# Modulation gates by way of the outer memory: computed in four column strips, written out, and read back across the partitions ahead of use

## The chip, the cores and the metric

The kernel runs on one core of one Trainium2 chip. The metric is the device time of one execution in microseconds (us). The engines are TensorE (PE; its weight loads are shown as PEld), VectorE (DVE), ScalarE (ACT), GpSimd (POOL) and SyncE (SP), which issues most of the transfers. The four compute engines each run their own instruction queue in order and wait for one another by semaphores.

## The reference

Two transformer blocks over x of shape (4, 1024, 256) in fp32, with 16 heads of width 16. The first block has windowed self-attention, cross-attention to 77 context rows in which each query keeps its 16 largest scores, and a gated MLP. Each of its three branches is multiplied by a gate that is computed from the conditioning vector, one row of 256 numbers for each of the 4 batches:

```python
m = silu(mod) @ w_ada + b_ada                      # (4, 9 * 256)
sh_msa, sc_msa, g_msa, sh_mca, sc_mca, g_mca, sh_mlp, sc_mlp, g_mlp = [m[:, i*C:(i+1)*C][:, None, :] for i in range(9)]
h = _self_attn(_ln(x) * (1 + sc_msa) + sh_msa, w_qkv, b_qkv, w_so, b_so)
x = x + h * g_msa
h = _topk_cross_attn(_ln(x) * (1 + sc_mca) + sh_mca, context, w_q, b_q, w_kv, b_kv, w_co, b_co)
x = x + h * g_mca
h = _swiglu(_ln(x) * (1 + sc_mlp) + sh_mlp, w_m1, b_m1, w_m2, b_m2)
x = x + h * g_mlp
```

The second block is plain cross-attention to the same context with its own modulation and without a gate.

## The kernel before

The work is cut into 16 units, four of 256 rows in each of 4 batches, and each unit goes through five stages: self-attention, the selection of the 16 largest scores, cross-attention, the MLP and the last attention. All operations of all units are first recorded, each with an engine, a cost, a priority and the buffers it reads and writes. A planner (`Plan.place`) then simulates the engines with these costs and picks an order; `issue` emits the instructions in that order, in one stream, so the recorded function of an operation puts all its instructions, whichever engine they belong to, at that operation's place in the order. Buffers come from small rings: two PSUM banks (`mm`) for nearly all dense products, two places for `gate`, two each for `w_so` and `w_co`, one for `w_m2`. A table of priorities (`ORDER`, `AHEAD`, `NUDGE`) shapes the plan.

A gate multiplies the columns of an output projection, so the kernel scales the weights once for each batch instead of every unit's result. `mod_gate` makes gate i for all 4 batches: two products of the conditioning (4 rows) with 256 columns of `w_ada` (L727), and a VectorE addition of the bias (L730) into `gates`, which has 4 partitions. `gated(b, ...)` then prepares batch b's three weights. For each, `w_so`, `w_co` or `w_m2` and its bias row are loaded, TensorE spreads the gate's row over 128 partitions by a product with a repeated column of the identity (L1303), ScalarE copies it from PSUM to one of the two `gate` places (L1306), and GpSimd multiplies the bias row (L1308) and the weight (L1310) by it. So there are 12 gates in all, 3 for each batch.

Other lines that matter below: L1011 and L1023 are GpSimd's steps of the normalization of an attention result, with ScalarE's L1008, L1013 and L1018 and VectorE's L1025 between them; L1035 is the output projection that uses the scaled weight; L1049 is GpSimd's addition of the scaled bias row to x; L907 and L909 are GpSimd's part of a layer norm; L961 to L965 split a shift into bf16 parts for TensorE (L970); L699 makes the other modulation rows, 32 columns of the array at a time in four strips; L821 is a layer norm of the context at the start; L1335 emits spare products where the plan has TensorE idle.

Of the kernel before, what the change touches and what calls it, by code (L numbers as in the profile page):

```python
# [9 lines left out]
F32 = mybir.dt.float32  # L10
BF16 = mybir.dt.bfloat16
AF = mybir.ActivationFunctionType
ALU = mybir.AluOpType
# [3 lines left out]
P = 128  # L17
# [371 lines left out]
def tile_block(ctx: ExitStack, tc: tile.TileContext, a: dict, out: bass.AP):  # L389
    nc = tc.nc  # L390

    x_d, cond_d, ctx_d = a["x"], a["cond_1024"], a["ctx_1024"]
    B, L, C = x_d.shape
# [3 lines left out]
    KC = C // P  # L397
# [21 lines left out]
    ident = ctile([P, P], "ident")  # L419
# [25 lines left out]
    for i in range(3):  # L445
        t = ctile([P, TU, 4, 32], f"parts{i}", BF16)
# [5 lines left out]
    for i in range(2):  # L452
        t = ctile([P, TU, H // 2, VP], f"v_self{i}")
# [3 lines left out]
    pl = Plan()  # L457
# [5 lines left out]
    def f_act(n):  # L463
        return 0.21 + 0.00081 * n

    def f_dve(n):
        return 0.155 + 0.00104 * n

    def f_pool(n):
        return 0.13 + 0.00222 * n  # L470
# [7 lines left out]
    T_GATE = ("D", "D", 0.22, 0.05, 0.37, 0.216)  # L478
# [11 lines left out]
    def fixed(name, shape, dt=F32):  # L490
        return pl.fixed(ctile(shape, name, dt), name)
# [7 lines left out]
    bp = fixed("bp", [P, C])  # L499
    n_mod = 26  # L500
    mod = fixed("mod", [P, n_mod, B])
    gates = fixed("gates", [B, 3, C])
    k_ctx = [fixed(f"k_{i}", [P, KC, B, 2, LC]) for i in range(2)]
    v_ctx = [fixed(f"v_{i}", [LC, B, H // 2, VP]) for i in range(2)]
    for v, fill in zip(v_ctx, (0.0, 1.0)):
# [7 lines left out]
    start, total = {}, 0  # L513
# [45 lines left out]
    at = Place(0)  # L559
# [3 lines left out]

    sc_t = at.buf("sc_t", [P, KC, 32])
    nc.gpsimd.memset(sc_t(), 0.0)
    bg_ada = at.buf("bg_ada", [B, 3, C])
    cx = at.buf("cx", [LC, B, C])
    cn = at.buf("cn", [LC, B, C])
    w_kv = [at.buf("w_kv0", [P, KC, 2 * C])]
# [3 lines left out]
    at = Place(start["slab"])  # L573
# [15 lines left out]
    def load(buf, src, kb, prio, key=None, eng="SP", view=None):  # L589
        def fn():  # L590
            dst = buf() if view is None else view(buf())
            (nc.sync if eng == "SP" else nc.scalar).dma_start(dst, src)
        pl.op(eng, f_dma(kb) if eng == "SP" else 0.3, fn, w=[buf if key is None else (buf, key)],
              prio=prio, lag=2.0)
# [8 lines left out]
    def row_bc(buf, name, lo, prio, key=None, view=None, np_=P):  # L603
        load(buf, a[name][lo : lo + C].partition_broadcast(np_), np_, prio, key, view=view)
# [11 lines left out]
    for g, names in enumerate(groups):  # L616
        for name, hi in names:
            n, r = hi // P, n_rows[g]
# [2 lines left out]
            col_of[name] = (g, r)  # L621
            n_rows[g] += n
    for i in range(3):
        row_bc(bg_ada, "L0_xcond_b_ada", (3 * i + 2) * C, (-79.5, -59.5, -49.5)[i], i, lambda t, i=i: t[:, i, :], B)
    row_bc(bv_self, "L0_xcond_b_qkv", 2 * C, -81)
    row_bc(bv_ctx[0], "L0_xcond_b_kv", C, -66)
    row_bc(bv_ctx[1], "L1_xcond_bkv", C, -29.5)
# [57 lines left out]
        nc.scalar.preload_act_table_set("natural_log_exp_and_others")  # L685
    pl.op("ACT", 1.5, silu, w=[sc_t], r=[pc], prio=-50, lag=-1.28)

    turn = [0]

    def mod_group(name, lo, m, scale_first, prio, dma_prio):  # L690
# [30 lines left out]
    def mod_gate(i, prio, dma_prio):  # L721
        c = chunk("L0_xcond_w_ada", (3 * i + 2) * C, C, dma_prio)
        pp = pl.buf("mm", f"modg{i}")

        def fn():
            for kc in range(KC):
                nc.tensor.matmul(pp()[:B, :C], sc_t()[:, kc, :B], c()[:, kc, :C],  # L727
                                 start=(kc == 0), stop=(kc == KC - 1))
        pl.op("PE", f_pe(C, 2), fn, w=[pp], r=[sc_t, c], prio=prio)
        pl.op("DVE", f_dve(256), lambda: nc.vector.tensor_tensor(  # L730
            gates()[:, i, :], pp()[:B, :C], bg_ada()[:, i, :], ALU.add), w=[(gates, i)], r=[pp, (bg_ada, i)], prio=prio)

    def filled(v):

# [67 lines left out]
    for q in range(4):  # L802
        lo = (q % 2) * HID + (q // 2) * 4 * P
# [7 lines left out]
    for b in range(B):  # L811
        pl.op("DVE", 0.42, lambda b=b: nc.vector.bn_stats(st_c()[:LC, b, :], cx()[:, b, :]),
              w=[(st_c, b)], r=[cx], prio=-1)
    for b in range(B):
        pl.op("DVE", 0.16, lambda b=b: nc.vector.bn_aggr(mv_c()[:LC, b, :], st_c()[:LC, b, :]),
              w=[(mv_c, b)], r=[(st_c, b)], prio=-1)
# [475 lines left out]
    def gated(b, pr):  # L1292

        gw = {}
        for i, (key, name, kc) in enumerate(
            (("so", "L0_xcond_w_so", KC), ("co", "L0_xcond_w_co", KC), ("m2", "L0_xcond_w_m2", NF))
        ):
            first = None if b else DMA_FIRST[i]
            w, row = pl.buf("w_" + key, f"w_{key}{b}"), pl.buf("row", f"b_{key}{b}")
            gate, pg = pl.buf("gate", f"gate{b}{i}"), pl.buf("mm", f"pg{b}{i}")  # L1300
            load(w, a[name].rearrange("(kc p) n -> p kc n", p=P), 128 * kc, first or pr)
            load(row, a[f"L0_xcond_b_{key}"].partition_broadcast(P), 128, first or pr)
            pl.op("PE:gate", T_GATE, lambda i=i, pg=pg: nc.tensor.matmul(  # L1303
                pg()[:, :C], ident[:B, b : b + 1].to_broadcast([B, P]), gates()[:, i, :], start=True, stop=True),
                w=[pg], r=[(gates, i)], prio=pr, take=[gate])
            pl.op("ACT:gate", f_act(256), lambda gate=gate, pg=pg: nc.scalar.copy(gate(), pg()[:, :C]),  # L1306
                  w=[gate], r=[pg], prio=pr)
            pl.op("POOL:gate", f_pool(256), lambda row=row, gate=gate: nc.gpsimd.tensor_tensor(  # L1308
                row(), row(), gate(), ALU.mult), w=[row], r=[row, gate], prio=pr)
            pl.op("POOL:gate", f_pool(256 * kc), lambda w=w, gate=gate, kc=kc: nc.gpsimd.tensor_tensor(  # L1310
                w(), w(), gate().unsqueeze(1).to_broadcast([P, kc, C]), ALU.mult),
                w=[w], r=[w, gate], prio=pr)
            gw["b_" + key], gw["w_" + key] = row, w
        return gw

# [60 lines left out]
```

## Time and profile before

| | |
|---|---|
| Median of 3 runs | 1040.41 us (1040.08 to 1044.87) |
| The profiled execution | 1041.43 us, span of its instructions 1039.4 us |
| TensorE busy, share of the span | 97%; VectorE 73%, ScalarE 70%, GpSimd 52% |
| Transfers | 27.01 MB, nearly all on SP's queue; DMA engines 70% busy in the first 52 us, then mostly idle |
| TensorE clock by fortieths of the span | 0.9 of full in the first slice, 0.7 in the second, then 0.9 or more |

In the profile, a line such as L1303 is the line of the kernel's source that recorded the instruction. A count such as x24 is of instructions; an fp32 product appears as two. What stands behind an arrow in brackets is the event that ended the idle time in front of an instruction. Busy times of TensorE include waiting inside its pipeline, so that a busy share near 100% shows that its queue is never empty, not that it works at its peak.

### The profile page before, as it was taken

To read this page: it belongs to the slowest core of one execution; us is meant where nothing else is said; L and a number is where in the kernel's file an instruction comes from. 1 tells how busy PE (TensorE), PEld (TensorE's weight loads), DVE (VectorE), ACT (ScalarE), POOL (GpSimd) and SP (SyncE) were. 2 spreads that over 40 slices of the span, in tenths; PEclk is the share of its full clock that TensorE was granted. 3 is DMA by queue.
4 is the path that set the end of the run, shared out by engine and by line. 5 is a ranking of instruction groups with operands and counts; after the bars stand their busy time and mean duration, and the time that the engine had idled before them with its cause. 6 is when DMAs were issued, how large, how long until landed. Compare 5 with 4: busy or idle time off the path is not lost.

```text
span 1039.4 us, 27476 instructions
## 1 busy us (share of the span) xinstructions
PE 1012.0 (97%) x10363; PEld 770.5 (74%) x10363; DVE 757.3 (73%) x4000; ACT 723.5 (70%) x1270; POOL 542.1 (52%) x751
## 2 busy tenths in 40 slices
PE   7899999999999999999999999999999999999997
PEld 5667777777777778777877777778767787778775
DVE  5177999979899999947833446599999977724232
ACT  3358786687687794758468667877688765764665
POOL 3384445466353573557635647546335464753653
PEclk9799999999999999999999999999999999999999
DMA  7710000001000000100000200000000001000000
GB/s 255 242 50 7 3 2 1 3 3 36 3 22 27 7 3 5 38 16 22 21 1 2 82 22 21 2 2 2 2 2 22 2 2 42 12 1 12 2 21 21
DMA packets 23623, 27.01 MB, mean 26 GB/s; under 512 B 1609, under 2 KB 20675, under 8 KB 23491
## 3 DMA queue, kind: packets, MB, share of 16 engines
q1 hardware_dynamic: 23455, 25.26, 7.7%
q8 instruction: 81, 1.33, 0.5%
q14 instruction: 52, 0.42, 0.1%
q10 hardware_dynamic: 35, 0.01, 0.0%
HBM read 21.07 MB, written 4.19 MB: 24 GB/s over the span
## 4 chain that ended last, share of the span: by engine, by line
PE 48%; DVE 13%; ACT 6%; POOL 2%; issue 1%; POOLq 0%; ACTq 0%; DVEq 0%
PE mm L1247 13%; PE mm L1275 8%; PE mm L938 5%; PE mm L1035 5%; PE s L1196 4%; PE o L1212 3%; PE s L985 3%; DVE share L1153 2%; DVE r L1147 2%; DVE nm L996 2%; PE s L1186 1%; DVE share L1145 1%; DVE share L1151 1%; PE mm L919 1%; ACT prob L1108 1%
## 5 line engine op out<-in xcount | busy, mean ns | idle before, releaser
L1247 PE MATMUL mm<-share,w_m 128*128 128x256 f32 x640 | 150.3, 386 | 0.4 <-ACT share L926 0.2
L1205 ACT ACTIVATE prob<-s 77x2048 f32<-77x2048 f32 x64 | 120.0, 1875 | 43.7 <-PE s L1201 43.4
L996 DVE TENSOR_REDUCE nm<-s 128x16 f32<-128x2048 f32 (+1 forms) x64 | 119.0, 1859 | 38.0 <-PE s L985 17.2
L1247 PEld LDWEIGHTS mm<-share,w_m 128*128 128x128 f32 x640 | 117.7, 190 | 26.0 <-issue 4.7
L1147 DVE MATCH_REPLACE8 r<-share 128x77 f32<-128x77 f32 x512 | 109.9, 222 | 0.0
L1145 DVE MAX8 share<-share 128x8 f32<-128x77 f32 x512 | 94.4, 225 | 21.0 <-ACT share L1138 21.0
L1153 DVE MATCH_REPLACE8 share<-share,r 128x77 f32<-128x77 f32 x512 | 109.6, 221 | 0.0
L1011 POOL TENSOR_TENSOR share<-share 128x256 f32<-128x256 f32 x64 | 47.1, 736 | 96.4 <-ACT share L1008 95.1
L1151 DVE MAX8 share<-r 128x8 f32<-128x77 f32 x512 | 93.9, 224 | 0.0
L1247 PE MATMUL mm<-slab,w_m 128*128 128x256 f32 x384 | 92.9, 388 | 0.7 <-ACT slab L926 0.5
L1023 POOL TENSOR_TENSOR slab<-slab,share 128x256 f32<-128x256 f32 x96 | 69.4, 730 | 28.4 <-ACT share L1018 19.2
L1261 POOL TENSOR_SCALAR slab<-slab 128x512 f32<-128x512 f32 x43 | 64.4, 1498 | 36.8 <-ACT slab L1259 33.0
L1247 PEld LDWEIGHTS mm<-slab,w_m 128*128 128x128 f32 x384 | 69.9, 190 | 15.6 <-issue 3.1
L1275 PE MATMUL mm<-share,slab 128*128 128x256 f32 x344 | 80.9, 381 | 0.0
L1008 ACT ACTIVATE share<-o,mask 128x256 f32<-128x256 f32 x128 | 66.6, 575 | 12.2 <-PE o L1212 9.6
L1108 ACT ACTIVATE prob<-s 128x2048 f32<-128x2048 f32 x32 | 60.5, 1889 | 17.9 <-PE s L1104 17.5
L1044 DVE TENSOR_TENSOR slab<-slab,mm 128x512 f32<-128x512 f32 x52 | 35.4, 680 | 50.9 <-PE mm L1035 25.7
L1275 PEld LDWEIGHTS mm<-share,slab 128*128 128x128 f32 x344 | 64.7, 190 | 10.0 <-issue 0.9
L1253 ACT ACTIVATE slab<-mm,cols 128x256 f32<-128x256 f32 x90 | 43.0, 480 | 41.0 <-PE mm L1247 40.5
L1212 PE MATMUL o<-prob,v 77*32 77x256 f32 x1024 | 67.9, 385 | 0.8 <-ACT share L1018 0.5
L1049 POOL TENSOR_TENSOR slab<-slab,row 128x512 f32<-128x512 f32 x39 | 49.9, 1278 | 28.5 <-DVE slab L912 15.4
L907 POOL TENSOR_SCALAR rs<-mv 128x2 f32<-128x2 f32 x64 | 14.2, 222 | 81.7 <-DVE mv L905 78.8
(183 smaller groups left out, 2427.0 us busy)
## 6 DMA issues: line engine op xcount, KB each, us to landing
share<-in_L_xcond_w_m_dram SPq DMA_DIRECT2D x4, 1024.0 KB
slab<-in_x_dram SPq DMA_DIRECT2D x9, 256.0 KB, 2.9
out_dram<-slab SPq DMA_DIRECT2D x9, 256.0 KB, 2.7
w_m<-in_L_xcond_w_m_dram SPq DMA_DIRECT2D x4, 512.0 KB, 6.8
share<-in_L_xcond_w_ada_dram SPq DMA_DIRECT2D x3, 512.0 KB, 3.8
w_so<-in_L_xcond_w_so_dram SPq DMA_DIRECT2D x4, 256.0 KB
w_co<-in_L_xcond_w_co_dram SPq DMA_DIRECT2D x4, 256.0 KB, 4.0
w_qkv<-in_L_xcond_w_qkv_dram SPq DMA_DIRECT2D x3, 256.0 KB
```

Source lines behind the costliest of these rows:

```text
L996: pl.op("DVE:max", f_dve(n), lambda: nc.vector.tensor_reduce(nm()[:, t], s4(), AX.X, ALU.max, negate=True), w=[(nm, t)], r=[s], prio=u.prio)
L1008: pl.op("ACT:nln", 0.5, lambda e=e, own=own, other=other: nc.scalar.activation(nz()[:, e, :], o()[:, ts(e, UT)], AF.Ln, bias=own, scale=ot ...
L1023: nc.gpsimd.tensor_tensor(dst, dst, shaped(nz()[:, k, :], dst), op)
L1108: pl.op("ACT:exp", f_act(2048), lambda s=s, prob=prob: nc.scalar.activation(prob(), s(), AF.Exp), w=[prob], r=[s], prio=pr)
L1145: nc.vector.max(top()[:, h + i, 0:8], sc()[:, h + i])
L1147: nc.vector.match_replace(r1()[:, i], top()[:, h + i, 0:8], sc()[:, h + i], NEG)
L1151: nc.vector.max(top()[:, h + i, 8:16], r1()[:, i])
L1153: nc.vector.match_replace(sc()[:, h + i], top()[:, h + i, 8:16], r1()[:, i], NEG)
L1205: pl.op("ACT:exp", f_act(2048), lambda s=s, prob=prob: nc.scalar.activation(prob()[:LC], s()[:LC], AF.Exp), w=[prob], r=[s], prio=pr)
L1212: nc.tensor.matmul(o()[r, :UT] if drops is not None else o()[r, ts(e, UT)], columns(v_z()[:, b], 8 * c + 2 * j + e), prob()[:LC, j, ts(e, ...
L1247: nc.tensor.matmul(pp()[:, ts(half, UT)], w_m1()[:, kc, m : m + P], ht()[:, kc, :], start=(kc == 0), stop=(kc == KC - 1))
L1275: nc.tensor.matmul(pp()[:, ts(t, C)], gts[f // 2]()[:, f % 2, ts(t, P)], w_m2()[:, f, :], start=(f == 0), stop=(f == NF - 1))
```

## The change

A gate is made in four column strips. The conditioning's 32 (padded) columns are multiplied with 64 columns of `w_ada` at a time, and strip j's result stands in partitions 32j to 32j + 3 of one PSUM tile; the bias, loaded in the same layout, is added to all 128 partitions at once. Right behind that addition, in the same recorded operation, GpSimd's queue gets four writes, one for each strip, to a tile of its own in the outer memory (`gates_d[i]`, 4 x 256). TensorE's spreading and ScalarE's copy stay in the plan with their costs, but emit nothing. In their stead GpSimd's queue reads the gate's row from the outer memory into all 128 partitions of the place that the plan gave it: the first two gates right after their writes, every later one as soon as the second multiplication by the gate that held the same place has been issued. The order of all other operations is the planner's, as before.

```diff
-    gates = fixed("gates", [B, 3, C])
+    gates = fixed("gates", [P, 3, C // 4])
+    dram = ctx.enter_context(tc.tile_pool(name="dram", bufs=1, space=bass.MemoryType.DRAM))
+    gates_d = [dram.tile([B, C], F32, tag=f"gates_d{i}", name=f"gates_d{i}") for i in range(3)]
...
-    bg_ada = at.buf("bg_ada", [B, 3, C])
+    bg_ada = at.buf("bg_ada", [P, 3, C // 4])
...
-        row_bc(bg_ada, "L0_xcond_b_ada", (3 * i + 2) * C, (-79.5, -59.5, -49.5)[i], i, lambda t, i=i: t[:, i, :], B)
+        lo = (3 * i + 2) * C
+        load(bg_ada, a["L0_xcond_b_ada"][lo : lo + C].rearrange("(j o n) -> j o n", j=4, o=1).to_broadcast([4, 32, C // 4]),
+             B, (-79.5, -59.5, -49.5)[i], i, view=lambda t, i=i: t[:, i, :])
...
+    gate_of = {}
+
+    def read_gate(n, place):
+        todo = [m for m in range(n, 3 * B) if gate_of[m]() is place]
+        if todo:
+            b, i = divmod(todo[0], 3)
+            nc.gpsimd.dma_start(place, gates_d[i][b, :].partition_broadcast(P))
...
             for kc in range(KC):
-                nc.tensor.matmul(pp()[:B, :C], sc_t()[:, kc, :B], c()[:, kc, :C],
-                                 start=(kc == 0), stop=(kc == KC - 1))
+                for j in range(4):
+                    nc.tensor.matmul(pp()[32 * j : 32 * j + 32, : C // 4], sc_t()[:, kc, :], c()[:, kc, ts(j, C // 4)],
+                                     start=(kc == 0), stop=(kc == KC - 1))
         pl.op("PE", f_pe(C, 2), fn, w=[pp], r=[sc_t, c], prio=prio)
-        pl.op("DVE", f_dve(256), lambda: nc.vector.tensor_tensor(
-            gates()[:, i, :], pp()[:B, :C], bg_ada()[:, i, :], ALU.add), w=[(gates, i)], r=[pp, (bg_ada, i)], prio=prio)
+
+        def add():
+            nc.vector.tensor_tensor(gates()[:, i, :], pp()[:, : C // 4], bg_ada()[:, i, :], ALU.add)
+            for j in range(4):
+                nc.gpsimd.dma_start(gates_d[i][:, ts(j, C // 4)], gates()[32 * j : 32 * j + B, i, :])
+            if i < 2:
+                read_gate(i, gate_of[i]())
+        pl.op("DVE", f_dve(256), add, w=[(gates, i)], r=[pp, (bg_ada, i)], prio=prio)
...
-            pl.op("PE:gate", T_GATE, lambda i=i, pg=pg: nc.tensor.matmul(
-                pg()[:, :C], ident[:B, b : b + 1].to_broadcast([B, P]), gates()[:, i, :], start=True, stop=True),
-                w=[pg], r=[(gates, i)], prio=pr, take=[gate])
-            pl.op("ACT:gate", f_act(256), lambda gate=gate, pg=pg: nc.scalar.copy(gate(), pg()[:, :C]),
-                  w=[gate], r=[pg], prio=pr)
-            pl.op("POOL:gate", f_pool(256), lambda row=row, gate=gate: nc.gpsimd.tensor_tensor(
-                row(), row(), gate(), ALU.mult), w=[row], r=[row, gate], prio=pr)
-            pl.op("POOL:gate", f_pool(256 * kc), lambda w=w, gate=gate, kc=kc: nc.gpsimd.tensor_tensor(
-                w(), w(), gate().unsqueeze(1).to_broadcast([P, kc, C]), ALU.mult),
-                w=[w], r=[w, gate], prio=pr)
+            gate_of[3 * b + i] = gate
+            pl.op("PE:gate", T_GATE, lambda: None, w=[pg], r=[(gates, i)], prio=pr, take=[gate])
+            pl.op("ACT:gate", f_act(256), lambda: None, w=[gate], r=[pg], prio=pr)
+            uses = []
+
+            def times_gate(t, g, n=3 * b + i, gate=gate, uses=uses):
+                nc.gpsimd.tensor_tensor(t, t, g, ALU.mult)
+                uses.append(t)
+                if len(uses) == 2:
+                    read_gate(n + 1, gate())
+            pl.op("POOL:gate", f_pool(256), lambda row=row, gate=gate, times_gate=times_gate: times_gate(row(), gate()),
+                  w=[row], r=[row, gate], prio=pr)
+            pl.op("POOL:gate", f_pool(256 * kc), lambda w=w, gate=gate, kc=kc, times_gate=times_gate: times_gate(
+                w(), gate().unsqueeze(1).to_broadcast([P, kc, C])), w=[w], r=[w, gate], prio=pr)
```

## The prediction

> **What bounds the kernel now.** I read the page first, then busy time by stretches, then the gate's own lines, then POOL in order of time, since POOL is where the change puts its new work.
>
> Page, busy time of each engine:
>
> ```profile
> PE 1012.0 (97%) x10363; PEld 770.5 (74%) x10363; DVE 757.3 (73%) x4000; ACT 723.5 (70%) x1270; POOL 542.1 (52%) x751
> ```
>
> Stretches (length, then busy of PE, PEld, DVE, ACT, POOL, then TensorE clock, DMA share, GB/s):
>
> ```profile
> 35.00:65.00 30.00, 28.44 (x243) 21.00 (x243) 10.62 (x38) 17.54 (x37) 21.12 (x23) 0.77 0.63 200
> 65.00:130.00 65.00, 62.39 (x816) 48.22 (x818) 57.38 (x253) 47.51 (x88) 33.12 (x55) 1.00 0.02 6
> 250.00:350.00 100.00, 97.41 (x1081) 72.37 (x1084) 95.73 (x562) 73.92 (x125) 44.08 (x75) 1.00 0.07 20
> 500.00:600.00 100.00, 98.96 (x951) 74.29 (x950) 46.78 (x157) 64.18 (x113) 54.11 (x74) 1.00 0.07 24
> ```
>
> TensorE is the bound, but DVE is nearly full too until about 350 us; after that TensorE stands alone. Between 35 and 65 us the clock is low and POOL, with 21.1 of 30 us, is busier than DVE or ACT.
>
> The lines of the gate's matmul and of its copy:
>
> ```profile
> L1303 PE MATMUL mm<-gates,ident x24: 372/454/791, 34.5 to 563.7; 4*128 4x256 f32 x24
> L1306 ACT COPY gate<-mm x12: 354/372/530, 35.2 to 567.4; 128x256 f32<-128x256 f32 x12
>   POOL row L1308: 22.4, 6
> ```
>
> Twelve gates, two matmul instructions and one copy each, all in the first 568 us; the last row says POOL waited 22.4 us, in six pieces, for those copies.
>
> POOL in order of time (start, length; in brackets its idle time before and who ended it):
>
> ```profile
> 23.88 0.26 POOL L965 TENSOR_TENSOR parts<-rest,parts 128x32 bf16<-128x32 f32 x1
> 35.63 0.72 POOL L1308 TENSOR_TENSOR row<-row,gate 128x256 f32<-128x256 f32 x1 [11.50 <-DMA w_m<-in_L_xcond_w_m_dram]
> ...
> 46.80 0.72 POOL L1308 TENSOR_TENSOR row<-row,gate 128x256 f32<-128x256 f32 x1
> 52.09 0.73 POOL L1011 TENSOR_TENSOR share<-share 128x256 f32<-128x256 f32 x1 [4.56 <-ACT share L1008]
> ...
> 55.36 0.86 POOL L1011 TENSOR_TENSOR share<-share 128x256 f32<-128x256 f32 x1 [1.44 <-ACT share L1008]
> ...
> 59.34 3.02 POOL L1023 TENSOR_TENSOR slab<-slab,share 128x256 f32<-128x256 f32 x4
> ```
>
> POOL is free from 24.1 to 35.6, multiplies three gates until 47.5, idles 4.6 us, then runs almost without a gap from 55.4 to 62.4, and TensorE's first output projection (L1035) starts at 63.8 after it. So POOL has some 4.6 + 1.4 us of slack ahead of a place where it sets TensorE's time.
>
> **The change part by part.** Numbers are against this execution (span 1039.4, its time 1041.43 us, 0.1% above the median 1040.41). About 0.5% (5.2 us) is what a measurement of this kernel can tell from no change.
>
> *TensorE loses the twelve gate matmuls.* From the timeline, start of the pair to start of what follows, less what the neighbour takes elsewhere: 0.58 (at 89.9), 0.41 (103.7), 0.35 (117.5), 0.62 (271.3), 0.53 (336.1), 0.53 (507.3), 0.63 (527.8), 0.62 (563.4): 4.3 us for eight. The five before 350 us (2.5) lie where DVE is nearly full; I take half, 1.25. The three after (1.8) I take at nine tenths, 1.6. Together -2.8; the ends are 0 (another engine is late instead) and -4.3. The four early gates (34.5 to 43.3) run at the low clock, about 0.85 and 1.0 us for the third and fourth on the way to the first weighted sums at 49.1; those 1.8 us count only if POOL is ready then (below).
>
> *ACT loses twelve copies* (12 x 0.372 = 4.5 us). Hidden behind TensorE where TensorE is the bound; where ACT's head waited for a gate (4.64 us at 507.9) the next work waits for the same TensorE order. I count 0; at best 1 us.
>
> *The three gates are computed in strips.* Before, four instructions in 0.8 to 1.0 us; the strips of L699 (16 instructions, 128 columns) take 0.64, so with 64 columns at most that. DVE's addition goes from 0.41 to some 0.2 (64 columns for 256). At 10 to 31 us these lie beside loads (TensorE still waits 1.4 us for a weight at 33.1): 0; without that cover -1. The bias loads become 128 pieces of 256 bytes: three issues on SP go from 0.27-0.39 to about the 0.47 of a 128-partition row load, +0.4 us on SP, which pauses from 20 to 29 anyway: 0, at worst +0.3. The smaller bias tile also moves the setup tiles behind it in the shared space; their last readers are done by 38.5 us, long before the rings laid over them are used: 0.
>
> *POOL issues 12 writes and 12 reads.* This is the disputed cost. No POOL DMA is in the trace. Nearest rows: SP's issues, 0.23 to 0.47 us each, and landing times of 2.5 to 2.9 us from issue (out_dram<-slab 2.5 and 2.7, slab<-in_x 2.9), 4.6 to 9.3 when the queues are full. The Trainium skill, "DMA: Bandwidth & Descriptors", section "SWDGE vs HWDGE vs iDMA", says that a DMA from GpSimd has its descriptors computed by that engine's own cores, where SP's are made by hardware; its section "Latency and other measured facts" prices the first at about 1 us ahead of the first byte, against 0.6. It speaks against this change, and no run here shows it. SP's row is another mechanism, so I take c = 1.0 us of POOL per DMA (an estimate from that page; ends 0.4 and 1.5), and l = 3 us to land (the write rows, a little more because the DMA share at 32 to 44 us is 0.88 to 0.99).
>
> The first gate is harmless: its addition ends at 11.8, POOL is idle until 20.7, and 5c + l = 8. Gates two and three are not. Their additions end at 29.8 and 31.4. POOL's queue then holds, in order: four writes, the read (which waits until they have landed, and everything behind it on POOL with it), four writes of the third gate, and only then the multiplication that now starts at 35.63. It starts at 29.85 + 9c + l = 41.85. The work up to the third row (POOL's own 10.4 us, the additions of L1049 included) now contains three reads: done at 40.25 + 12c + l = 55.25, where it was 47.5. The 4.6 us of slack is gone; the first L1011 starts at 55.25 instead of 52.09, and who waits for it are ACT's L1013, DVE's L1025 and then L1023. The second L1011 follows 1.7 us later (56.95 for 55.36); the run of 7.0 us to the end of L1023 gets one more read, ending at 64.95 where it was 62.36: **+2.6 us** at TensorE's first projection, which later work inherits almost whole. With c = 0.4, l = 2.5 POOL is ready at 47.6, the chain starts as early as TensorE allows, and this becomes -1.8 + 0.4 = -1.4; with c = 1.5 it is +9.1. It turns from gain to loss near c = 0.8.
>
> *Later reads.* Six, each about 1 us of POOL right behind the weight's multiplication. At 424 and 533 POOL has 6.4 and 1.5 us of idle time behind: 0. At 96.6 the next L1011 is 0.8 late, with 1.8 idle after it: +0.3. At 237.9, 0.55 idle ahead of a queue: +0.2. At 335.2 the read comes 2.0 us before its use at 337.25; it lands near 338.8, and L961 at 338.93, on which TensorE waits, goes to 339.5: +0.5. At 510.4 L907 is 1.0 late: +0.3. Together +1.3, ends +0.3 and +2.5. What replaces the 22.4 us of POOL's waits for the copies is mostly nothing, as the reads are old by then (9 of 12 by over 9 us); POOL just idles further on, so 0.
>
> Sum: -2.8 + 2.6 + 1.3 = +1.1 us, hence 1041.5 on the median.
>
> A second rule bears on the loss. The Trainium skill, "TensorE: Matmul & The Clock Gate", Part 1, says that an idle window of about 3.4 us halves the clock until a busy one has passed. Here the clock is 0.50 at 36 to 48 us though TensorE counts as busy for all of 40 to 48, so recovery takes longer than the rule says. A stall of 2.6 us at 63 us would cost nothing more by the rule; one of 9 us would cost 2 to 5 us on top.
>
> **The rivals.** *Faster (0.20):* POOL's issues cost what SP's do. Then -1.4 early, TensorE's full -4.3, later +0.3, ACT -0.5: -5.9, that is 1034.5. For it: after 500 us TensorE is 99% busy with nothing else near it. Against: DVE's 95.7 of 100 us where five gates lie.
> *Slower (0.35):* POOL's queue at 29.8 us is the bound. From c = 1.3 the early term is +6.5 or more and the total passes +5; at c = 1.5 it is +8, with the clock up to +13, about 1050. Its far end: if each strip's write waits for the landing of the one before (their rows in the outer memory interlace), a gate costs 4(c + l) = 16 us of POOL and the first multiplication starts past 70, some +30: 1070. For it: the queue is in order and the slack only 6 us. Against: the strips' addresses are disjoint.
> *It does not do what it says (0.03):* the reads stand so close to their use that POOL waits for them as it did for copies; true of 335 us alone by the order above, +0.5 each, still about 1042.
>
> **How the numbers follow.** The likeliest case (0.42) has c between 0.6 and 1.25: 1037.5 to 1045.5, point 1041.5; with the third rival 0.45 within 0.5%. Faster 0.20, slower 0.35. For 8 in 10 the range takes most of the faster case (to 1033.5) and the slower one without its far end (to 1053).
>
> **What would show it.** L1303 and L1306 gone from TensorE and ACT; POOL DMA rows of about 1 us; the first L1308 near 42; the first L1011 near 55; L1035 near 66 with TensorE idle before it; after 500 us the stretch shorter by 1 to 2 us. L1308 before 37 would make the slow step wrong; L1308 past 50 would make the forecast too low.

## The result and the profile after

The changed kernel takes 1049.18 us (median of 4 runs, 1048.32 to 1050.61), the kernel before 1040.63 us (4 runs, 1040.08 to 1044.87): a ratio of 1.0081, 95% interval 1.0062 to 1.0100. It is slower by more than the 0.5% that can be told from no change. The spans of the two profiled executions, 1047.5 and 1039.4 us, differ by 8.1 us, and this is what has to be explained.

The first part of the page says little: TensorE lost 5.8 us of busy time and POOL gained 14.7 us.

```profile
PE 1006.2 (96%) x10375; PEld 768.4 (73%) x10375; DVE 760.0 (73%) x4000; ACT 720.2 (69%) x1258; POOL 556.8 (53%) x775
```

(The 24 spreading instructions are gone from TensorE, but the strips of the gates brought 36 new ones.) Two stretches say where to look. Columns: length, busy time of PE, PEld, DVE, ACT, POOL, TensorE clock, DMA share, GB/s:

```profile
35.00:65.00 30.00, 20.10 (x211) 14.97 (x212) 7.36 (x28) 13.83 (x27) 21.13 (x24) 0.73 0.68 219
65.00:130.00 65.00, 61.56 (x755) 48.28 (x754) 56.91 (x249) 43.95 (x80) 37.99 (x60) 1.00 0.04 10
```

Between 35 and 65 us TensorE was busy for 20.1 of 30 us instead of 28.4, and POOL was as busy as before: POOL did its work, but at other times.

To find the rest I matched the instructions of the two traces, one by one for each engine, and took start after less start before. The difference, of single profiled executions:

| at (us of before) | after less before | what happens there |
|---|---|---|
| 45 to 50 | -2 to -2.7 (TensorE) | TensorE ahead, without the gates' products |
| 60, then 64 | +6.2, +5.5 | POOL late at the first normalization (L1034) |
| 64 to 236 | +5.5, constant | the spreading products at 89.9, 103.7 and 117.5, now gone, give nothing |
| 240, 260 | +8.6, +7.6 | one subtraction of VectorE, see below |
| 340, 364 | +8.4, +8.8 | POOL waits for the read of a gate, see experiment 2 |
| 507 | +8.0 | the product at 507.3 gone: -0.8 |
| to the end | +8.0 | the products at 527.8 and 563.4 give nothing |

The lines of the source have moved: in the changed kernel L751 issues the writes of a gate and L702 the reads, L1333 is both multiplications by a gate (L1308 and L1310), L1034 and L1046 are the steps of the normalization (L1011 and L1023), L1072 is the addition of the bias row (L1049), L930, L932 and L935 are the layer norm (L907, L909 and L912), and L806 is VectorE's bias addition that takes a product of the context out of PSUM (L783). In the kernels of the experiments they move by a few lines more.

The DMAs of the change, issue durations (min/median/max, ns) and landing:

```profile
L751 POOL DMA_DIRECT2D gates_d<-gates x12: 515/521/767, 11.9 to 39.9; - x12
L702 POOL DMA_DIRECT2D gate<-gates_d x12: 582/635/654, 19.9 to 532.9; - x12
gates_d<-gates POOLq DMA_DIRECT2D x12, 1.0 KB, 6.1
gate<-gates_d POOLq DMA_DIRECT2D x12, 128.0 KB, 3.3
```

A write occupies POOL for 0.52 us and a read for 0.64, but a write of 1 KB needs a median of 6.1 us to land. What that does shows in POOL in order of time, in the stretch that the prediction was about (start, length; in brackets the idle time before and who ended it):

```profile
30.01 2.16 POOL L751 DMA_DIRECT2D gates_d<-gates  x4 [5.91 <-DVE gates L749]
37.77 0.58 POOL L702 DMA_DIRECT2D gate<-gates_d  x1 [5.61 <-DMA gates_d<-gates]
38.34 2.05 POOL L751 DMA_DIRECT2D gates_d<-gates  x4
40.41 0.74 POOL L1333 TENSOR_TENSOR row<-row,gate 128x256 f32<-128x256 f32 x1
41.10 1.27 POOL L1333 TENSOR_TENSOR w_so<-w_so,gate 128x512 f32<-128x512 f32 x1
46.75 0.62 POOL L702 DMA_DIRECT2D gate<-gates_d  x1 [4.38 <-DMA bp<-in_L_xcond_bp_dram]
...
55.95 0.73 POOL L1333 TENSOR_TENSOR row<-row,gate 128x256 f32<-128x256 f32 x1
56.97 0.58 POOL L702 DMA_DIRECT2D gate<-gates_d  x1 [0.30 <-POOL row L1333]
57.57 0.73 POOL L1034 TENSOR_TENSOR share<-share 128x256 f32<-128x256 f32 x1
58.40 0.23 POOL L930 TENSOR_SCALAR rs<-mv 128x2 f32<-128x2 f32 x1
58.71 0.73 POOL L932 TENSOR_TENSOR rs<-rs,mhalf 128x2 f32<-128x2 f32 x1
```

There are two waits of a read for its own gate's writes, with everything else of POOL behind each: 5.61 us at 32.2, and 4.38 us at 42.4. The second is put down to a load (`bp`), which the trace shows landing at 46.69. The third gate's last write was issued at 39.87 and landed at 46.18, so at least 3.8 of the 4.38 us are the wait for the writes.

Who waits for POOL there is not only the normalization. L932 is the step of the next unit's layer norm, and VectorE's queue stands behind it:

```profile
51.93 0.42 DVE L806 TENSOR_TENSOR v<-mm,share 77x256 f32<-77x256 f32 x1 [2.61 <-ACT k L794]
59.48 1.13 DVE L935 TENSOR_SCALAR slab<-slab,mv,rs 128x256 f32<-128x256 f32 x2 [7.13 <-POOL rs L932]
60.52 0.41 DVE L806 TENSOR_TENSOR v<-mm,share 77x256 f32<-77x256 f32 x1
```

The second L806 would free a PSUM bank for TensorE, but it is queued behind L935, which waits for POOL. So TensorE has nothing to do from 53.6 to 61.0 us:

```profile
60.99 1.11 PE L942 MATMUL mm<-ident,slab 128*128 128x128 f32 x4 [7.43 <-DVE v L806]
```

And its clock falls (columns as in the stretches above):

```profile
44.00:48.00 4.00, 4.00 (x87) 3.17 (x86) 1.06 (x3) 1.45 (x1) 1.24 (x2) 0.94 0.99 309
56.00:60.00 4.00, 0.00 (x0) 0.00 (x0) 0.53 (x1) 0.42 (x1) 3.51 (x7) 0.77 0.42 117
60.00:64.00 4.00, 3.01 (x9) 2.30 (x10) 2.82 (x12) 1.44 (x3) 3.31 (x4) 0.50 0.01 2
```

The first of these rows shows the side of the change that works: TensorE has its clock back at 44 to 48 us, where the trace of before shows 0.50 until 48. The gain is spent on waiting for POOL.

The second step, at 240 us, is a single instruction of VectorE, the subtraction behind the selection of the 16 largest scores. Before, VectorE and then the POOL instruction beside it, which began while the subtraction ran and took 0.90 us instead of 0.73:

```profile
240.26 0.41 DVE L1158 TENSOR_TENSOR share<-share 128x256 f32<-128x256 f32 x1
```

```profile
240.36 0.90 POOL L1011 TENSOR_TENSOR share<-share 128x256 f32<-128x256 f32 x1
```

After, VectorE and then POOL at the same time:

```profile
245.71 3.58 DVE L1181 TENSOR_TENSOR share<-share 128x256 f32<-128x256 f32 x1
```

```profile
243.62 0.65 POOL L702 DMA_DIRECT2D gate<-gates_d  x1 [0.30 <-POOL w_so L1333]
244.30 1.28 POOL L1072 TENSOR_TENSOR slab<-slab,row 128x512 f32<-128x512 f32 x1
245.54 0.73 POOL L1046 TENSOR_TENSOR slab<-slab,share 128x256 f32<-128x256 f32 x1
246.23 0.72 POOL L1034 TENSOR_TENSOR share<-share 128x256 f32<-128x256 f32 x1
246.91 0.72 POOL L1046 TENSOR_TENSOR slab<-slab,share 128x256 f32<-128x256 f32 x1
247.60 0.72 POOL L1034 TENSOR_TENSOR share<-share 128x256 f32<-128x256 f32 x1
248.29 0.72 POOL L1046 TENSOR_TENSOR slab<-slab,share 128x256 f32<-128x256 f32 x1
```

The subtraction starts inside an unbroken run of POOL and ends 0.28 us after the run does. The read at 243.6 stands 2.1 us ahead of the subtraction. The Trainium skill, "SBUF — State Buffer", section "Who interferes with whom", says that a VectorE instruction with two operands in SBUF and a GpSimd instruction that reads SBUF lock each other out for a whole instruction, and that the order of issue decides who waits. The trace of before agrees: the subtraction there ends 0.28 us after the POOL instruction that it began beside. After the change it waits for five instructions, not one.

### The profile page after: what moved, and what is told of

Read it like the earlier page. It is cut to its first block, busy times and chain, and to the rows that moved or that the text cites. A ratio compares the mean times of both kernels' runs of the same rounds, so it can differ in the third digit from the quotient of the medians.

```text
span 1047.5 us, 27517 instructions
## 1 busy us (share of the span) xinstructions
PE 1006.2 (96%) x10375; PEld 768.4 (73%) x10375; DVE 760.0 (73%) x4000; ACT 720.2 (69%) x1258; POOL 556.8 (53%) x775
## 4 chain that ended last, share of the span: by engine, by line
PE 44%; DVE 15%; ACT 5%; POOL 3%; issue 2%; DMA 1%; POOLq 0%; ACTq 0%; DVEq 0%
PE mm L1270 12%; PE mm L1298 7%; PE mm L961 5%; PE mm L1058 5%; PE s L1219 3%; PE o L1235 3%; PE s L1008 3%; DVE r L1170 3%; DVE share L1176 3%; DVE share L1168 2%; DVE share L1174 2%; PE mm L942 1%; PE s L1209 1%; PE mm L1098 1%; DVE slab L935 1%
## 5 line engine op out<-in xcount | busy, mean ns | idle before, releaser
L1034 POOL TENSOR_TENSOR share<-share 128x256 f32<-128x256 f32 x64 | 46.9, 733 | 86.3 <-ACT share L1031 81.7
L1046 POOL TENSOR_TENSOR slab<-slab,share 128x256 f32<-128x256 f32 x96 | 69.6, 732 | 38.6 <-ACT share L1041 19.1
L1072 POOL TENSOR_TENSOR slab<-slab,row 128x512 f32<-128x512 f32 x39 | 49.9, 1280 | 30.2 <-DVE slab L935 17.1
L930 POOL TENSOR_SCALAR rs<-mv 128x2 f32<-128x2 f32 x64 | 14.3, 224 | 91.7 <-DVE mv L928 88.9
```

The costliest lines, as they stand in the source:

```text
L1046: nc.gpsimd.tensor_tensor(dst, dst, shaped(nz()[:, k, :], dst), op)
```

## The experiments

Two explanations were to be tested. The one of the early stretch (theory 1 in the expectations): the transfers cost about 6 to 7 us because POOL's queue stands behind reads that wait for slowly landing writes, while the removal of products and copies is worth some 3 to 5 us by itself. The one of the step at 240 us (theory 3): a read that is issued by POOL moves POOL's instructions so that they hold VectorE's subtraction. All shifts below are starts against the profiled execution of before, as in the table above. The first four kernels were timed against a median of before of 1042.09 us (7 runs), the next three against 1041.95 us (39 runs), the last against 1041.07 us (27 runs).

**1. The changed kernel without its transfers.** The 24 DMAs are left out, and with them the gates' values: both places are filled with ones.

```diff
-            for j in range(4):
-                nc.gpsimd.dma_start(gates_d[i][:, ts(j, C // 4)], gates()[32 * j : 32 * j + B, i, :])
-            if i < 2:
-                read_gate(i, gate_of[i]())
+            if i == 0:
+                for n in range(2):
+                    nc.gpsimd.memset(gate_of[n](), 1.0)
...
-                if len(uses) == 2:
-                    read_gate(n + 1, gate())
```

> The changed kernel without its 24 transfers: both gate places are filled once with ones, so the multiplications by the gates use ones. It shows what taking the matmuls and copies away is worth when nothing takes their place. Theory 1 (the loss is POOL's in-order queue between 30 and 50 us; TensorE's freed time is worth nothing after 65 us, as the two traces keep a constant distance there): the work near 62 us starts 1 to 2.5 us earlier than in the kernel before, and nothing is gained later but about 1 us near 507: 1037 to 1039.5. The prediction's view (freed TensorE time carries): 4 to 5 us, 1036 or less.

Measured: 1036.76 us (1036.01 to 1037.43), ratio 0.9954 (0.9938 to 0.9971); span 1033.9, 5.5 us below before. The shift is -4.4 us already by 52 us, stays there but for small steps, goes to -5.6 at 508 and ends at -5.5. So the removal is worth 5.5 us of span, of which 4.4 come from the four early gates and about 1 from the eight later ones: between the two expected values, larger early and smaller late than I had it. The windows show the early part, in the low-clock stretch:

```profile
40.00:44.00 4.00, 4.00 (x64) 3.22 (x64) 0.09 (x1) 1.88 (x1) 2.39 (x1) 0.79 1.05 362
44.00:48.00 4.00, 4.00 (x80) 2.85 (x76) 2.09 (x7) 3.25 (x5) 3.24 (x3) 1.00 0.91 246
```

Before, the same two windows:

```profile
40.00:44.00 4.00, 4.00 (x47) 3.26 (x46) 0.00 (x0) 2.00 (x2) 3.82 (x3) 0.50 0.88 305
44.00:48.00 4.00, 4.00 (x27) 2.90 (x30) 0.50 (x1) 0.51 (x2) 3.53 (x2) 0.50 0.83 259
```

TensorE's clock returns some 7 us earlier. Why taking away eight small instructions does this was not tested. POOL is ready too: its first normalization starts at 47.61 (52.09 before).

**2. The kernel before with the transfers added.** Gates by TensorE and ScalarE as before; the same 12 writes and 12 reads on POOL, the reads into 96 partitions that nothing uses.

```diff
+            for j in range(4):
+                nc.gpsimd.dma_start(gates_d[i][:, ts(j, C // 4)], gates()[:B, i, ts(j, C // 4)])
+            if i < 2:
+                read_gate(i, gate_of[i]())
...
+                if len(uses) == 2:
+                    read_gate(n + 1, gate())
```

> The kernel before with the 24 transfers added on POOL's queue at the same places; the reads go to 96 spare partitions that nobody uses, and the gates still come from TensorE and ACT. Theory 1 (POOL's queue): POOL waits twice for writes to land, the first multiplication starts near 40, the third row ends near 56, and the first projection (66 in the changed kernel) is 5 to 6 us late; with the step near 240 us the total is 1046 to 1050. Rival (strips, bias loads or the missing TensorE work cause the loss): 1040 to 1042, since none of these is in this kernel.

Measured: 1048.78 us (1047.88 to 1049.38), ratio 1.0067 (1.0052 to 1.0082); span 1046.6. The shift is +6.2 at 64 us, +8.2 at 240, and 7.2 from 272 us to the end: both steps of the change are here, with no strips and no product removed. POOL waits in the same two places:

```profile
39.00 0.54 POOL L698 DMA_DIRECT2D gates<-gates_d  x1 [6.05 <-DMA gates_d<-gates]
...
48.61 0.57 POOL L698 DMA_DIRECT2D gates<-gates_d  x1 [5.07 <-DMA bp<-in_L_xcond_bp_dram]
```

So the transfers bring both steps by themselves. The third loss of the change, +1.2 at 335 to 364 us, is not here: the shift stays at 7.2. There the changed kernel waits for the read itself, which was issued at 343.32, too close to its use:

```profile
346.64 0.72 POOL L1333 TENSOR_TENSOR row<-row,gate 128x256 f32<-128x256 f32 x1 [2.66 <-DMA gate<-gates_d]
```

In this kernel the gate comes from ScalarE, and POOL waits 1.41 us for it. The two parts do not add up (-5.5 and +7.2 make +1.7, the change has +8.1), above all since early, where POOL is the bound, TensorE's lead is worth only 6.2 - 5.5 = 0.7 us instead of 4.4; the rest is this third loss and a step at 240 us of 1.0 us net here and 2.1 there.

**3. The second gate's read behind the first gate's multiplications.** The two multiplications by the first gate then stand ahead of the wait.

```diff
-            if i < 2:
-                read_gate(i, gate_of[i]())
+            if i == 0:
+                read_gate(0, gate_of[0]())
...
                 if len(uses) == 2:
+                    if n == 0:
+                        read_gate(1, gate_of[1]())
                     read_gate(n + 1, gate())
```

> The changed kernel with one move: the read of the second gate is issued behind the first gate's two multiplications instead of ahead of them, so that the four writes of the third gate and the first multiplications do not stand behind the wait for the second gate's writes. The number of transfers is the same. Theory 1 (waiting for the landing costs, not issuing): the first row is multiplied near 34.5 to 36 instead of 40.4, the third row is done near 51, the early loss of 5.5 us becomes 0 or a gain of up to 2; the step near 240 stays or not by chance of phase: 1039 to 1043. Rival (issuing 24 transfers on POOL is the cost): 1046 or more, as all are still issued.

Measured: 1047.2 us (1046.22 to 1047.27), ratio 1.0050 (1.0035 to 1.0065); span 1045.5. Early the shift is +3.5 us, where theory 1 had expected none: a miss. The trace shows why:

```profile
34.03 0.74 POOL L1333 TENSOR_TENSOR row<-row,gate 128x256 f32<-128x256 f32 x1
...
37.32 0.62 POOL L702 DMA_DIRECT2D gate<-gates_d  x1 [1.34 <-DMA gates_d<-gates]
39.06 0.56 POOL L702 DMA_DIRECT2D gate<-gates_d  x1 [1.11 <-DMA gates_d<-gates]
44.66 0.72 POOL L1333 TENSOR_TENSOR row<-row,gate 128x256 f32<-128x256 f32 x1 [5.05 <-DMA gate<-gates_d]
```

The waits for writes are down to 1.34 and 1.11 us, and the first multiplication is at 34.0, as expected. But then the read itself takes 7.3 us from issue to use (37.32 to 44.66), and POOL waits 5.05 us for it. The rival's number (1046 us or more) came true, its cause (the time for issuing) did not: the issues take 0.52 to 0.62 us each, and POOL stands idle. It is the round trip, write and read, of 12 to 14 us under the loads that has to fit ahead of the second gate's use. The step at 240 us is here as well: +7.0 after 3.8, the subtraction at 3.57 us.

**4. All transfers on SP's queue.** The reads stand where the plan has the spreading product.

```diff
-                nc.gpsimd.dma_start(gates_d[i][:, ts(j, C // 4)], gates()[32 * j : 32 * j + B, i, :])
+                nc.sync.dma_start(gates_d[i][:, ts(j, C // 4)], gates()[32 * j : 32 * j + B, i, :])
...
-            pl.op("PE:gate", T_GATE, lambda: None, w=[pg], r=[(gates, i)], prio=pr, take=[gate])
+            pl.op("PE:gate", T_GATE, lambda b=b, i=i, gate=gate: nc.sync.dma_start(
+                gate(), gates_d[i][b, :].partition_broadcast(P)), w=[pg], r=[(gates, i)], prio=pr, take=[gate])
```

> The changed kernel with all 24 transfers on SP's queue, each read at the place in the order where the gate's matmul stood. POOL only multiplies. Theory 1: the early loss goes, and the step near 240 with it, since POOL's queue there is as before: 1037 to 1041. Rival (the round trip itself is too slow, whichever queue carries it, or SP's waits for landing make the weights and x late behind it): first multiplications past 38, or late loads of x, and 1045 or more.

Measured: 1048.67 us (1046.89 to 1052.29), ratio 1.0071 (1.0047 to 1.0094); span 1044.9, shift +6.1 at 64 us. (The profiled execution is the fastest of the four.) The rival held. The first read is issued at 37.68, where the plan has the product, and POOL can use it only 7.6 us later, so that it gets its first gate later than ever. And SP stands: the last of the three reads in this row was issued at 47.22, after POOL had multiplied `w_so` (45.93 to 47.20) and so freed the place that it fills, and the loads stand behind it:

```profile
37.68 9.86 SPq L1326 DMA_DIRECT2D gate<-gates_d  x3
```

```profile
45.25 0.73 POOL L1332 TENSOR_TENSOR row<-row,gate 128x256 f32<-128x256 f32 x1 [20.20 <-DMA gate<-gates_d]
```

This is what the Trainium skill says of it in "DMA: Bandwidth & Descriptors", section "Anatomy of one DMA — SWDGE (gpsimd) path": a transfer waits for a semaphore in the queue that issues it, ahead of dispatch (here for 8.5 us, from 38.7 to 47.2). Its fixed cost of about 2 us is not what the runs show under load: 5 to 7 us for a write of 1 KB by POOL. On SP's queue the same writes landed sooner, by the semaphore records of this trace: 1.1 to 1.2 us after their issue at 11.8 to 12.8 us, where windows of 1 us show a DMA share of 0.08 at most, and 3.7 to 4.1 us after their issue at 33.6 to 34.6, at a share of 0.72 to 0.97. So under the loads a write is slow on either queue; how much of POOL's 5 to 7 us lies in its own path is open, as POOL issued no write in a quiet stretch. At 240 us this kernel, which has no read on POOL, loses almost nothing: the subtraction there takes 0.89 us.

**5. A delay of POOL at 238 us in the kernel before.** Two fillings of unused partitions behind the third batch's `w_so`, in place of the read.

```diff
+                if n == 6:
+                    nc.gpsimd.memset(gates()[32:64], 0.0)
+                    nc.gpsimd.memset(gates()[32:64, 0], 0.0)
```

> The kernel before with nothing but two POOL memsets of unused partitions (together about 1 us) behind the multiplication of the third batch's w_so, at 237.9 us; POOL idles 0.55 us there, so its queue shifts by about 0.4 us. In the changed kernel a read stands there, and VectorE's subtraction of L1158 (two operands in SBUF) took 3.58 us where it took 0.41 before. Theory 3 (the subtraction meets POOL's queue at another phase and is held off until POOL's run of back-to-back instructions ends): the same subtraction takes 2 us or more here too and the total rises by 1 to 3 us, to 1042.5 to 1044.5. Rival (the transfer itself, its descriptors or its writes into SBUF hold VectorE): the subtraction stays near 0.4 us and the total rises by 0.5 us at most.

Measured: 1042.03 us (1040.48 to 1046.90), ratio 0.9999 (0.9985 to 1.0013). A miss: the subtraction takes 0.66 us (at 242.71), not 2 or more. POOL's own instruction beside it was the longer one:

```profile
243.05 0.92 POOL L1011 TENSOR_TENSOR share<-share 128x256 f32<-128x256 f32 x1
```

VectorE was served inside the run here, as before the change, so a delay of POOL by about 1 us is not by itself the cause. (The profiled execution is 5 us longer than that of before; 3 us of it lie at 288 to 297 us, where two windows of 4 us show a clock of 0.73 and 0.50. The timed runs show no difference.)

**6. One read of the changed kernel on SP.** Only the eighth gate's, the one at 243.6 us.

```diff
-            nc.gpsimd.dma_start(place, gates_d[i][b, :].partition_broadcast(P))
+            (nc.sync if todo[0] == 7 else nc.gpsimd).dma_start(place, gates_d[i][b, :].partition_broadcast(P))
```

> The changed kernel with one of its 24 transfers, the read of the eighth gate (the one behind w_so of the third batch, near 243 us), issued by SP instead of POOL. Theory 3 (phase of POOL's queue): the step of about 2.5 us between 236 and 260 us goes, the subtraction takes about 0.4 us, the total falls by 1.5 to 2.5 us below the changed kernel, to 1046 to 1047.5. Rival (the transfer itself, or something else of the change): the step stays and the total is 1048.5 or more.

Measured: 1046.96 us (1046.23 to 1050.15), ratio 1.0045 (1.0027 to 1.0063); span 1045.0, 2.5 us below the changed kernel. The shift goes from 5.4 to 5.4 across 240 us, and the subtraction is short:

```profile
244.97 0.75 DVE L1181 TENSOR_TENSOR share<-share 128x256 f32<-128x256 f32 x1
```

So this one read costs about 2.5 us when POOL issues it, 2.1 us ahead of a subtraction that does not use it. That it acts by moving POOL's run (theory 3) is not shown. Of the 32 subtractions in each of the ten traces, only three outlast more than one POOL instruction: this one in the changed kernel and in experiments 2 and 3, each 2.1 to 2.5 us behind a read issued by POOL. Wherever else one was held, it ended 0.28 to 0.30 us after the end of a single POOL instruction. How far the POOL instruction beside it had got when the subtraction began does not tell the two groups apart: 0.17, 0.18 and 0.54 us where it was held, 0.35, 0.59 and 0.60 us into one of the same kind where it was let in. So something of the issuing itself may hold VectorE; no run separates that from the shift, and the cause stays open.

**7. More time for the round trip.** The second gate's read as in 3; the third gate is read into a place of its own, and its multiplications are held until just ahead of the sixth gate's row (by 98 us); reads from the sixth gate on by SP.

```diff
+    place_2 = ctile([P, C], "place_2")
+    held = []
...
-            nc.gpsimd.dma_start(place, gates_d[i][b, :].partition_broadcast(P))
+            (nc.gpsimd if todo[0] < 5 else nc.sync).dma_start(place, gates_d[i][b, :].partition_broadcast(P))
...
+                if n == 2:
+                    held.append((t, place_2.unsqueeze(1).to_broadcast([P, NF, C]) if len(t.shape) == 3 else place_2))
+                    return
+                if n == 5 and not uses:
+                    for h, hg in held:
+                        nc.gpsimd.tensor_tensor(h, h, hg, ALU.mult)
...
+                    if n == 0:
+                        read_gate(1, gate_of[1]())
+                        nc.gpsimd.dma_start(place_2, gates_d[2][0, :].partition_broadcast(P))
+                    read_gate(max(n + 1, 3), gate())
```

> A version meant to keep the gain and not the loss: the changed kernel, with the second gate's read behind the first gate's multiplications, the third gate read into a place of its own and multiplied only ahead of the sixth gate's (near 102 us, where POOL idles; its weight is first used near 161), and the reads from the sixth gate on issued by SP. Theory 1 (the early loss is POOL's queue standing between the landings of the round trip and the first attention's normalization): POOL is free for the normalization by 47 to 48, the stretch to 62 us is 2.5 to 4.4 us shorter than in the kernel before, as in the kernel without transfers, and nothing is lost near 240: 1036.5 to 1039.5. Rival (the round trip costs wherever it stands, by its traffic among the weight loads): 1042 or more.

Measured: 1041.59 us (1039.82 to 1042.91), ratio 0.9990 (0.9976 to 1.0004); span 1038.1. Early it does what was expected: POOL's first normalization is at 48.28 and the shift is -3.0 from 64 us on. At 100 us it falls to -0.4. In POOL stands the held multiplication, in VectorE the subtraction:

```profile
98.18 4.54 POOL L1340 TENSOR_TENSOR share<-share,place 128x2048 f32<-128x2048 f32 x1
```

```profile
100.00 3.00 DVE L1183 TENSOR_TENSOR share<-share 128x256 f32<-128x256 f32 x1
```

It begins in the middle of POOL's instruction and ends 0.3 us after it, 3.00 us instead of 0.41. The expected total was missed by this, and it is the cleanest view of such a lock: VectorE waits for one instruction, as the page cited above has it.

**8. The held multiplications where both engines leave room.** The bias row behind an addition at 132.8 us, the weights behind one that ends at 139.7 us (times of the trace of kernel 7), where POOL was idle for 4.6 us and VectorE has no such subtraction.

```diff
-                if n == 5 and not uses:
-                    for h, hg in held:
-                        nc.gpsimd.tensor_tensor(h, h, hg, ALU.mult)
...
             nc.gpsimd.tensor_tensor(dst, dst, shaped(nz()[:, k, :], dst), op)
+            turns_n.append(k)
+            for h, hg in held:
+                if len(turns_n) == (16 if len(h.shape) == 3 else 13):
+                    nc.gpsimd.tensor_tensor(h, h, hg, ALU.mult)
```

> The kernel of the held third gate, with one thing moved: its two multiplications no longer stand ahead of the sixth gate's row at 98 us, where the large one held VectorE's subtraction for 3.0 us and the lead fell from 3.0 to 0.4 us, but where POOL idled in that kernel's trace: the row behind an attention addition at 132.8 us (the next work of POOL came at 137.4) and the weights (4.54 us) behind the multiplication that ended at 139.7 us (the next came at 144.3). VectorE has no subtraction of two SBUF operands there. If the loss at 100 us was POOL's long instruction against VectorE's subtraction, the subtraction at about 100 us is back at 0.41 us, the lead of 3.0 us stays to the end, the 0.9 us at 507 us come on top, and the end is about 4 us ahead of before: 1036.5 to 1038.5 us, a ratio of 0.995 to 0.9975, below both kernels. Rival: the lead is lost anyway at the next meeting of engines (the wait at 100 us was for something else, or the weights held back to 144 us make the first MLP late), 1040 us or more, with the loss seen between 100 and 165 us.

Measured: 1039.27 us (1036.12 to 1040.96), ratio 0.9971 (0.9961 to 0.9982), inside the expected ratio; the median is 0.8 us above the expected times. The subtraction is back, and the weight fits the gap:

```profile
100.54 0.41 DVE L1187 TENSOR_TENSOR share<-share 128x256 f32<-128x256 f32 x1
```

```profile
137.65 4.54 POOL L1052 TENSOR_TENSOR share<-share,place 128x2048 f32<-128x2048 f32 x1
142.30 0.22 POOL L932 TENSOR_SCALAR rs<-mv 128x2 f32<-128x2 f32 x1
```

The shift is -2.5 us from 64 to 284 us with no loss at 100 or 240, then 1.4 us are lost at 288 to 296, and 0.9 gained at 507; the span is 1037.7. The loss at 288 us goes with a lower clock, 0.75 and 0.82 in two windows of 4 us where before has 1.00:

```profile
284.00:288.00 4.00, 3.52 (x36) 2.09 (x29) 4.00 (x16) 4.00 (x13) 1.86 (x3) 0.75 0.00 0
288.00:292.00 4.00, 4.00 (x27) 2.93 (x26) 2.72 (x15) 2.61 (x8) 1.26 (x3) 0.82 0.00 0
```

Nothing of the gates lies there, and kernel 7 keeps its clock at the same place; what brings the drop stays open. This version is below both kernels: by 0.29% of before, less than the 0.5% asked for in the prediction, but with an interval that excludes no change.

## Why the prediction was wrong on the point, and where it was right

It forecast 1041.5 us with 0.45 on no change; 1049.18 us is within its range and is its rival "slower", which had 0.35.

- **The mechanism was right.** POOL's queue from 29.8 us is the bound, in the order that was written down: four writes, a read that waits with everything behind it, four writes, then the first multiplication. That multiplication came at 40.41 (41.85 forecast), the first gate's own wait of 5.67 us was harmless (POOL's next work came at 20.66), the third row ended at 56.7 (55.25), and TensorE had an idle stretch ahead of its first projection.
- **The step that failed is the landing time in the early term**, +2.6 forecast, +5.5 measured. It took c = 1.0 us of POOL for each DMA and l = 3 us once. Measured are c = 0.52 (writes) and about 0.6 (reads), and a wait of 5.61 us. A second wait, of 4.38 us, was not in the sum at all: the third gate's read stands behind writes that were issued only at 38.3 to 40.4, and I let it pass. Up to the third row the rows show eight writes and three reads, one read fewer than the sum has (the fourth follows at 56.97, still ahead of L1034). With the measured numbers the formula gives 40.25 + 8 x 0.52 + 3 x 0.6 + 5.61 + 4.38 = 56.2, and the rows have 56.7, with 0.3 us idle ahead of the read at 49.65. The waits were 7.0 us longer than l and the issues 6.0 us shorter than 12c, so that it is luck that 55.25 came so near. The sum also lacks a wait of 0.56 us for VectorE (L935) ahead of L1072 at 60.68; with it L1046 ends at 67.87 (64.95 forecast). The 1 us ahead of the first byte that the prediction took from the Trainium skill was used as time of POOL, where the rows show 0.52 to 0.65 us; and l was taken from rows of quiet times, though the DMA share of 0.88 to 0.99 was on the page, and with it rows of 4.6 to 9.3 us for full queues. Those were the nearer rows.
- **Who waits** was only half named: the normalization (L1011, now L1034) was; VectorE's queue behind the next unit's layer norm (7.13 us at L935) was not, and it is what kept TensorE idle. That TensorE's first output projection waits for the end of POOL's run was misread: L1035 starts 1.4 us after L1023 has ended, and 0.39 us after another product of TensorE. After the change it starts at 70.01 (66 forecast), 2.1 us after the end of L1046, again 0.39 us after TensorE's own work.
- **TensorE, early:** 1.8 us "only if POOL is ready then". POOL was not, and all but 0.7 us of it went unused. With POOL ready it is worth 4.4 us (experiment 1): 1.2 us is the fourth gate's pair of products at 42.1, and some 2.4 us are the products behind it at the full clock (the eight of L1075 take 2.25 us instead of 3.78, the next 32 of L1098 take 1.17 instead of 2.04).
- **TensorE, later:** -2.8 forecast, -0.8 measured (at 507 us), and some -1 in experiment 1. Half for the gates beside a full VectorE was too much: at 89.9, 103.7, 117.5, 271 and 336 us nothing came. The two at 527.8 and 563.4, counted at nine tenths where TensorE is 98% busy and nothing else is near, gave nothing either; why is not settled.
- **Later reads:** +1.3 forecast. At 96.6 the measured cost is 0 (0.3 forecast), around 335 to 364 us 1.2 (0.5; the wait for the read's landing was named rightly, 2.66 us of it), and at 237.9, forecast at 0.2, it is 2.1 net, or 2.5 by experiment 6. The prediction asked only what stands behind the read in POOL's queue. What made the loss at 240 us was on VectorE.
- **ACT's copies and the strips** at 0: experiment 1 contains both and shows no shift but the early one and 507; experiment 2 changes neither and shows both of the larger losses.
- **The clock rule:** the prediction doubted it and put 2 to 5 us on a stall of 9 us. TensorE's stall of 7.4 us did bring the clock to 0.50 at 60 to 64 us, 0.88 in the next window and 1.00 after. It shows on TensorE, which is 4.95 us late at L942 (60.99 for 56.04) and 6.2 at 66.00. But POOL's L1046 ends 5.5 us late (67.87 for 62.36) and the layer norm behind it too (L935 at 69.02 for 63.50), and from 75 us on everything is 5.5 us late: the low clock lay beside POOL's work and cost nothing that stays.
- **The rivals:** "slower" was tied to c of 1.3 us or more; it came true at half of that, through l. Its far end, strips that wait for one another, did not occur: four issues take 2.16 us and one landing. "Faster" would have needed POOL to be ready, which experiments 7 and 8 approach with -3.0 and -2.5 us early.

Sum of what was measured: +5.5 early, +2.1 at 240 us, +1.2 at 335 to 364, -0.8 at 507, together 8.0 of the 8.1 us of span.

## What to carry to other kernels

When a value goes by way of the outer memory, count the round trip from rows of the same stretch with the same DMA share, and count it once for every read that stands behind a write; an in-order queue makes each of its waits one of all that is behind it, on POOL's queue and on SP's. Put the wait where nothing urgent follows, and give the last reader the slack: moving the reads and two multiplications, with no less work, turned 0.8% slower into 0.3% faster. And before an engine gets more work, look at what its neighbour runs at that moment, not only at what waits for it.

## What the runs showed of the hardware

- In the changed kernel a write of 1 KB from SBUF to the outer memory, issued by POOL, landed 5.1 to 7.0 us after its issue in the first 47 us, where most windows of 4 us show a DMA share of 0.8 to 1.0; on SP's queue (experiment 4) it took 1.1 to 1.2 us at a share of 0.08 or less and 3.7 to 4.1 us at 0.72 to 0.97. A read of 128 KB took 3.2 to 3.3 us in quiet times and up to 6.7 (7.3 in experiment 3) under the loads.
- VectorE's subtraction of two SBUF operands, 0.41 us, took 3.00 us beside one long POOL instruction (experiment 7), and 3.58, 3.57 and 2.53 us beside five short ones in a row (the changed kernel, experiments 3 and 2; in the last it was let in ahead of the fifth), each time with a read issued by POOL 2.1 to 2.5 us before. Beside the same run without such a read it took 0.41 to 0.89 us. What the read has to do with it is not known from these runs.
- The granted clock fell to 0.5 to 0.8 for 4 to 8 us near 290 us in two of the nine other kernels (experiments 5 and 8; the rest and before show 1.00), for 3.0 and 1.4 us of time, with nothing different in the instructions there.
